# A decoder layer: unit-long score accumulation, row maxima turned through DRAM, and reciprocals of sums spread over partitions by DMA

## The chip, the cores and the metric

One core of one Trainium2 chip runs the whole kernel. The metric is the device time of one execution in microseconds. Beside it the profiler records one execution: its span is the time from the first to the last instruction. The engines are TensorE (PE, with its weight loads PEld), VectorE (DVE), ScalarE (ACT), GpSimd (POOL), and SP, whose queue issues the DMAs.

## The reference

Two sequences of 2048 tokens with 512 features pass through three residual parts. The first is self-attention with 16 heads of 32 features, rotary angles and a softmax over all 2048 keys:

```python
x = x + attn(layernorm(x), W_q, W_k, W_v, W_o)      # softmax(rope(Q) rope(K)^T / sqrt(32)) V, then W_o
x = x + xattn(layernorm(x), ctx, ctx)               # gelu(x ctx^T) ctx, 77 context rows
x = x + clip(layernorm(x) @ sign(W_f)^T * scale + bias, -100, 100)
```

All inputs and outputs are float32.

## The kernel before

**Units, steps, half-steps.** For each batch `project_batch` computes keys, queries and values; then `Attention.run` works through 32 units. A unit is one group `g` of four heads (128 features), one half (256 queries) of a query block `qb`. It has 8 steps; a step takes 256 of the keys (two chunks of 128) for all four heads, and is done in two half-steps of two heads each. The order of TensorE, VectorE, ScalarE and GpSimd within the attention is the one in which the program writes it; SP's order is the scheduler's.

**A half-step on the engines.** TensorE computes the scores of two heads (`scores`, L565), transposed, with keys on partitions, into the banks `st`. Between them it computes plain scores for the *other* two heads of a unit that comes later (`maxima`, L472, three banks `ps`, two used per half-step), which VectorE reduces to row maxima (L484). ScalarE takes the exponential of `st` (L705), GpSimd adds the two chunks (L707), and TensorE multiplies by the values (`weigh`, L583) and, one step later, sums over the keys with a matrix of ones (`total`, L597), both into one bank `acc`. The maxima run `AHEAD` = 10 steps ahead of the scores.

**Scores by differences.** A bank `st` is not cleared from step to step. `lower` (L550) puts the negated row maximum of each query into the bank, as a product of ones with a row `mrow` that holds the maximum in three bfloat16 parts; then step 0 adds the scores of keys in block 0, and each later step adds the product with the *difference* of two key blocks (`dk`), so that the bank holds the new block's scores less the maximum. Steps 0 to 3 do this for the first half of each of the four key blocks, steps 4 to 7 for the second half; so `lower` runs in steps 0 and 4, and clears the banks.

**The maxima's rows.** `split_maxima` takes the negated maximum on VectorE (L491) and splits it in three parts on GpSimd (L493 to L497); `turn_maxima` turns the 128 x 256 tile `mt` with a transposing DMA on SP (L504). For a batch's first unit TensorE turns it (L508).

**Dividing.** `divide` is a generator of which `finish` takes one piece per half-step. After a unit's last totals ScalarE copies `acc` to `num` (L611); VectorE inverts the sums, which stand in 32 equal rows per head, in two pieces of 128 x 128 (L617), and GpSimd multiplies (L620) into the place of the queries. After the last group of a query block, `after_attention` (output projection L382, context part L389 and L408, feed-forward L363, transposes L345) is queued as background, of which a piece is taken at some half-steps.

**Pools.** `work` has 5 tiles of 128 x 512 that `num` shares with the background work; `sums` has 3 tiles `sm`; the angles `cos` and `sin` have their own.

Of the kernel before, what the change touches and what calls it, by code (L numbers as in the profile page):

```python
# [9 lines left out]
F32 = mybir.dt.float32  # L10
F32R = mybir.dt.float32r
BF16 = mybir.dt.bfloat16
# [4 lines left out]
P = 128  # L17
# [11 lines left out]
AHEAD = STEPS + 2  # L29
# [7 lines left out]
def decoder_layer(  # L37
# [51 lines left out]
    cos = const.tile([P, NCH, DK // 2], F32, tag="cos", name="cos")  # L89
    sin = const.tile([P, NCH, DK // 2], F32, tag="sin", name="sin")  # L90
    nc.sync.dma_start(cos, rope_cos.rearrange("(p c) d -> p c d", p=P))
    nc.sync.dma_start(sin, rope_sin.rearrange("(p c) d -> p c d", p=P))
# [13 lines left out]
    mts = []  # L106
    for n in range(2):
        mt = const.tile([P, 2, 4, DK], BF16, tag=f"mt{n}", name=f"mt{n}")
        nc.vector.memset(mt, 0.0)
        mts.append(mt)  # L110
# [69 lines left out]
    def project_batch(b, ahead, att, xnt, wk, wq, wv):  # L180
# [26 lines left out]
        def rotate(ch, a, ps, r):  # L207
            half = [P, H, DK // 2]
            cs = cos[:, ch, None, :, None].to_broadcast(half + [2])
            sn = sin[:, ch, None, :].to_broadcast(half)  # L210
# [234 lines left out]
    class Attention:  # L445
# [53 lines left out]

        def turn_maxima(self, u):  # L500
            mt = mts[u % 2]
            mrow = small.tile([P, 2, P], BF16, tag="mrow", name="mrow")
            if u > 0:
                nc.sync.dma_start_transpose(mrow, mt.rearrange("p c h d -> p (c h d)"))  # L504
            else:
                pt = ps_s.tile([P, 2, P], BF16, tag="s", name="ptm")
                for c in range(2):
                    nc.tensor.transpose(  # L508
                        pt[:, c, :], mt[:, c].rearrange("p h d -> p (h d)"), ident_b
                    )  # L510
                nc.vector.tensor_copy(mrow, pt)
            self.mrow[u] = mrow.rearrange("p c q -> p (c q)")
# [3 lines left out]
        def key_steps(self):  # L516
            self.dk = [None] + [
                const.tile([P, ND, BLK], F32, tag=f"w{n}", name=f"dk{n}") for n in "kqv"
            ]

# [15 lines left out]
            queue.append(others())  # L536

# [21 lines left out]
        def scores(self, u, i, heads, c):  # L559
            qb, g, hf = self.units[u]  # L560
            kb, kc = divmod(self.chunk(i, c), CPB)
            keys = self.dk[kb] if kb else self.k[kb]
            for h in heads:
                r = self.rows[h]
                nc.tensor.matmul(  # L565
                    self.st[h][:, c, :],
                    keys[r, g, kc * P : (kc + 1) * P],
                    self.q[qb][r, g, hf * HQ : (hf + 1) * HQ],
                    start=False,
                    stop=True,  # L570
                    skip_group_check=True,
                )
# [34 lines left out]
        def divide(self, u):  # L607
# [7 lines left out]
            for c in range(2):  # L615
                part = slice(c * P, (c + 1) * P)
                nc.vector.reciprocal(num[:, 1, part], num[:, 1, part])  # L617
                if not last:
                    yield
                (nc.vector if last else nc.gpsimd).tensor_mul(  # L620
                    self.q[qb][:, g, hf * HQ + c * P : hf * HQ + (c + 1) * P],
                    num[:, 0, part],
                    num[:, 1, part],
                )
# [22 lines left out]
        def run(self):  # L647
# [37 lines left out]
            for t in range(NU * STEPS):  # L685
# [12 lines left out]
                for heads, others in (((0, 1), (2, 3)), ((2, 3), (0, 1))):  # L698
                    if i % NB == 0:
                        self.lower(u, heads)  # L700
                    self.scores(u, i, heads, 0)
# [8 lines left out]
                    if heads[0] == 0:  # L710
                        first_half()
                        finish()
                        if u >= NU - ND:
# [3 lines left out]
                    else:  # L717
# [20 lines left out]
    for b in range(B):  # L738
        att = Attention(b)
        project_batch(b, x_next, att, xnt, *qkv)  # L740
# [4 lines left out]
        if b + 1 < B:  # L745
            x_next = att.x_next
            qkv = load_qkv()
    alone.append(True)
# [51 lines left out]
```

## Time and profile before

| | |
|---|---|
| median of 3 runs | 2693.01 us (2692.51 to 2693.29) |
| the profiled execution's own time | 2693.15 us |
| its span | 2691.0 us |
| mean granted TensorE clock | 0.998 |
| TensorE busy | 2668.3 us (99%) |
| VectorE busy | 1710.0 us (64%) |
| ScalarE busy | 1321.0 us (49%) |
| GpSimd busy | 1732.8 us (64%) |
| a unit without background work | 31.09 us |

In the page's groups, the text before the bar names line, engine, operation, output and inputs with their shapes and the count; behind it stand busy time, the mean duration of one in ns, and the engine's idle time before them with what ended it. In a timeline the columns are start and duration in us, engine, line, operation and count. A float32 product is recorded as two instructions. "L" with a number is a line of the kernel before unless said otherwise.

### The profile page before, as it was taken

The numbers are of one execution on the slowest core, as the hardware profiler recorded it, in microseconds if no ns is written. First come the engines' busy times: TensorE is split into PE (matmuls) and PEld (weight loads), VectorE is DVE, ScalarE is ACT, GpSimd is POOL, SyncE is SP. The second block draws the span as 40 slices with busy tenths as digits, with TensorE's granted clock in tenths as the row PEclk, the third lists the DMA queues.
The fourth block names the chain that finished last, engine by engine and source line by source line (L and its number), as shares of the span: only waits on it lengthen the run. The fifth ranks groups of instructions, "written<-read, shape, count | busy, mean of one in ns | idle before, by whom it ended". The sixth has DMA issues, their size and how long they took to land.

```text
span 2691.0 us, 70222 instructions
## 1 busy us (share of the span) xinstructions
PE 2668.3 (99%) x30756; PEld 1490.3 (55%) x30756; DVE 1710.0 (64%) x2863; ACT 1321.0 (49%) x2394; POOL 1732.8 (64%) x1876
## 2 busy tenths in 40 slices
PE   8999999999999999999999999999999999999998
PEld 4445555555555555555554455555565555555555
DVE  3447777676766766676344477766767667766754
ACT  2115555455546554555422155555555455546553
POOL 3227777567857785677543287766687567857772
PEclk9999999999999999999999999999999999999999
DMA  3010000000000000000201000000000000000000
GB/s 126 24 32 2 5 4 4 4 4 18 20 3 4 12 28 3 4 12 26 73 25 40 5 4 4 4 4 4 4 27 12 4 4 19 19 4 4 19 19 17
DMA packets 38019, 43.54 MB, mean 16 GB/s; under 512 B 20662, under 2 KB 20918, under 8 KB 37712
## 3 DMA queue, kind: packets, MB, share of 16 engines
q1 hardware_dynamic: 37712, 39.05, 4.8%
q8 instruction: 241, 3.95, 0.6%
q14 instruction: 66, 0.54, 0.1%
HBM read 26.58 MB, written 8.39 MB: 13 GB/s over the span
## 4 chain that ended last, share of the span: by engine, by line
PE 98%; DVE 1%; DMA 0%; issue 0%; ACT 0%; POOL 0%; SPq 0%; POOLq 0%; ACTq 0%
PE st L565 23%; PE acc L583 22%; PE ps L472 18%; PE acc L597 8%; PE po L382 4%; PE pk L183 4%; PE pq L183 4%; PE pv L183 4%; PE st L550 3%; PE pf L363 2%; PE pt L345 1%; PE po L408 1%; PE ptqk L191 1%; PE ph L389 1%; PE pt L173 1%; DMA wk<-in_wk_t_dram 0%
## 5 line engine op out<-in xcount | busy, mean ns | idle before, releaser
L707 POOL TENSOR_TENSOR sm<-pw 128x512 f32<-128x512 f32 x1024 | 1295.2, 1272 | 599.5 <-ACT pw L705 596.8
L484 DVE TENSOR_REDUCE mx<-ps 128x1 f32<-128x512 f32 x2048 | 1308.9, 682 | 513.0 <-PE ps L472 509.1
L705 ACT ACTIVATE pw<-st 128x512 f32<-128x512 f32 x2048 | 1111.4, 595 | 947.0 <-PE ps L472 619.4
L472 PE MATMUL ps<-k,q 32*128 32x512 f32 x4096 | 1187.8, 640 | 0.0
L583 PE MATMUL acc<-pw,v 128*32 128x256 f32 x8192 | 655.1, 391 | 0.0
L597 PE MATMUL acc<-sm,ones 128*32 128x128 f32 x7680 | 388.8, 280 | 0.0
L583 PEld LDWEIGHTS acc<-pw,v 128*32 128x32 f32 x8192 | 162.5, 108 | 396.6 <-issue 378.3
L472 PEld LDWEIGHTS ps<-k,q 32*128 32x128 f32 x4096 | 352.4, 183 | 20.2 <-issue 13.8
L597 PEld LDWEIGHTS acc<-sm,ones 128*32 128x32 f32 x7680 | 248.6, 110 | 153.2
L565 PE MATMUL st<-q,dkk 32*128 32x256 f32 x2048 | 291.2, 400 | 0.0
L565 PE MATMUL st<-q,dkq 32*128 32x256 f32 x2048 | 290.0, 400 | 0.0
L565 PE MATMUL st<-q,dkv 32*128 32x256 f32 x2048 | 290.0, 400 | 0.0
L565 PE MATMUL st<-q,k 32*128 32x256 f32 x2048 | 262.8, 375 | 0.0
L565 PEld LDWEIGHTS st<-q,dkk 32*128 32x128 f32 x2048 | 175.8, 184 | 89.5 <-issue 51.3
L565 PEld LDWEIGHTS st<-q,dkq 32*128 32x128 f32 x2048 | 173.0, 184 | 79.9 <-issue 54.1
L565 PEld LDWEIGHTS st<-q,dkv 32*128 32x128 f32 x2048 | 175.0, 184 | 58.6 <-issue 26.3
L565 PEld LDWEIGHTS st<-q,k 32*128 32x128 f32 x2048 | 195.4, 187 | 14.0
L219 POOL TENSOR_TENSOR r<-r 128x512 f32<-128x512 f32 x64 | 81.1, 1268 | 161.8 <-DVE r L218 151.5
L617 DVE RECIPROCAL num<-num 128x128 f32<-128x128 f32 x128 | 120.4, 942 | 53.5 <-ACT num L611 53.5
L137 DVE BATCH_NORM_STATS2 st<-x 128x6 f32<-128x512 f32 x96 | 65.4, 686 | 91.7 <-DMA x<-in_x_dram 91.4
L183 PE MATMUL pk<-wk,xnt 128*128 128x512 f32 x256 | 118.2, 606 | 2.4 <-ACT xnt L175 1.3
L382 PE MATMUL po<-wo,q 128*128 128x512 f32 x256 | 117.4, 603 | 0.0
(109 smaller groups left out, 1784.9 us busy)
## 6 DMA issues: line engine op xcount, KB each, us to landing
x<-in_x_dram SPq DMA_DIRECT2D x64, 256.0 KB, 2.8
out_dram<-x SPq DMA_DIRECT2D x32, 256.0 KB, 2.0
wk<-in_wk_t_dram SPq DMA_DIRECT2D x2, 1024.0 KB, 7.8
wq<-in_wq_t_dram SPq DMA_DIRECT2D x2, 1024.0 KB, 9.9
wv<-in_wv_t_dram SPq DMA_DIRECT2D x2, 1024.0 KB, 5.5
wo<-in_wo_t_dram SPq DMA_DIRECT2D x1, 1024.0 KB, 9.9
wf<-in_wf_t_dram SPq DMA_DIRECT2D x1, 1024.0 KB, 5.0
mrow<-mt SPq DMA_TRANSPOSE x62, 2.3
```

The costliest lines, as they stand in the source:

```text
L183: nc.tensor.matmul(dst, xnt[:, i, :], w[:, i, :], start=(i == 0), stop=(i == ND - 1))
L219: nc.gpsimd.tensor_add(r[:, 0, a], r[:, 0, a], r[:, 1, a])
L382: nc.tensor.matmul(ps, ot[:, i, cols], wo[:, i, :], start=(i == 0), stop=(i == ND - 1))
L472: nc.tensor.matmul(ps, self.q[qb][self.rows[h], g, q0 : q0 + P], self.k[kb][self.rows[h], g, :], start=True, stop=True,)
L484: nc.vector.tensor_reduce(mx[:, qc, h, kb : kb + 1], ps, AX.X, ALU.max)
L550: nc.tensor.matmul(self.st[h], ones_b[r, :], mrow[r, None, :].to_broadcast([DK, 2, HQ]), start=True, stop=False, skip_group_check=True,)
L565: nc.tensor.matmul(self.st[h][:, c, :], keys[r, g, kc * P : (kc + 1) * P], self.q[qb][r, g, hf * HQ : (hf + 1) * HQ], start=False, stop=Tr ...
L583: nc.tensor.matmul(acc[self.rows[h], 0, :], self.v[self.chunk(i, c)][:, d0 : d0 + DK], pw[:, h, c, :], start=(i == 0 and c == 0), stop=(i ...
L597: nc.tensor.matmul(acc[self.rows[h], 1, part], ones, sm[:, h, part], start=False, stop=(i == STEPS - 1), skip_group_check=True,)
L617: nc.vector.reciprocal(num[:, 1, part], num[:, 1, part])
L705: nc.scalar.activation(pw[:, h], self.st[h], AF.Exp, scale=SCALE)
L707: nc.gpsimd.tensor_add(sm[:, hs, :], pw[:, hs, 0, :], pw[:, hs, 1, :])
```

## The change

**One `lower` per unit.** Step 4 no longer starts over from block 0: it adds the product with the difference of block 0's second half and the last block's first half. This difference, `wrap` (128 x 256), is made by GpSimd at step 0 of a unit whose group is not the last one's.

**The maxima's rows.** The three parts are made on VectorE, in two pieces, a half-step apart; `mt` shrinks to 128 x 32, VectorE transposes it in 32 x 32 blocks, one DMA stores the result to DRAM, and eight DMAs gather each head's three rows into `mrow`. `AHEAD` becomes 11, and the turning begins five half-steps before the row is used. The first unit still uses TensorE.

**The reciprocals.** Four DMAs spread a row of 256 sums of each head over its 32 partitions (`share`, 128 x 8); three half-steps later VectorE inverts that, four DMAs gather it to one row per head (`once`, a `work` tile), four more spread the row to 32 partitions of `num`, and four half-steps later GpSimd multiplies once. The very last unit divides as before.

**The angles** share a buffer with `sm` (`load_angles`) and are loaded for each batch.

```diff
-AHEAD = STEPS + 2
+AHEAD = STEPS + 3
-    cos = const.tile([P, NCH, DK // 2], F32, tag="cos", name="cos")
-    sin = const.tile([P, NCH, DK // 2], F32, tag="sin", name="sin")
-    nc.sync.dma_start(cos, rope_cos.rearrange("(p c) d -> p c d", p=P))
-    nc.sync.dma_start(sin, rope_sin.rearrange("(p c) d -> p c d", p=P))
+    def load_angles():
+        angles = sums.tile([P, 2, NCH, DK // 2], F32, tag="sm", name="angles")
+        for n, table in enumerate((rope_cos, rope_sin)):
+            nc.sync.dma_start(angles[:, n], table.rearrange("(p c) d -> p c d", p=P))
+        return angles
...
         def split_maxima(self, u):
...
-            mt = mts[u % 2]
-            nc.gpsimd.tensor_copy(mt[:, :, :, 0], neg)
-            nc.gpsimd.tensor_tensor(neg, neg, mt[:, :, :, 0], ALU.subtract)
-            nc.gpsimd.tensor_copy(mt[:, :, :, 1], neg)
-            nc.gpsimd.tensor_tensor(neg, neg, mt[:, :, :, 1], ALU.subtract)
-            nc.gpsimd.tensor_copy(mt[:, :, :, 2], neg)
+            if u == 0:
+                parts = [first_mt[:, :, :, n] for n in range(3)]
+            else:
+                by_head = mts[u % 2][:, :, 0:6].rearrange("p h (c n) -> p c h n", n=3)
+                parts = [by_head[:, :, :, n] for n in range(3)]
+            nc.vector.tensor_copy(parts[0], neg)
+            nc.vector.tensor_tensor(neg, neg, parts[0], ALU.subtract)
+            self.rest = neg, parts
 
         def turn_maxima(self, u):
-            mt = mts[u % 2]
-            mrow = small.tile([P, 2, P], BF16, tag="mrow", name="mrow")
-            if u > 0:
-                nc.sync.dma_start_transpose(mrow, mt.rearrange("p c h d -> p (c h d)"))
+            neg, parts = self.rest
+            nc.vector.tensor_copy(parts[1], neg)
+            nc.vector.tensor_tensor(parts[2], neg, parts[1], ALU.subtract)
+            mrow = mrows[u % 2]
...
+                square = small.tile([P, DK], BF16, tag="square", name="square")
+                nc.vector.transpose(square, mts[u % 2].rearrange("p h n -> p (h n)"))
+                rows = dram.tile([P, DK], BF16, tag="rows", name="rows")
+                nc.sync.dma_start(rows, square)
+                by_row = rows.rearrange("(a h n) i -> n a h i", a=4, h=4)
+                for h in range(4):
+                    for c in range(2):
+                        nc.sync.dma_start(
+                            mrow[h * DK : h * DK + 3, c].rearrange("n (a i) -> n a i", a=4),
+                            by_row[3 * c : 3 * c + 3, :, h, :],
+                        )
...
+        def wrap_around(self, g):
+            if self.wrap is None or self.wrap[0] != g:
+                d = small.tile([P, BLK // 2], F32, tag="wrap", name="wrap")
+                nc.gpsimd.tensor_sub(
+                    d, self.k[0][:, g, BLK // 2 :], self.k[NB - 1][:, g, : BLK // 2]
+                )
+                self.wrap = g, d
...
-            keys = self.dk[kb] if kb else self.k[kb]
+            if i == NB:
+                keys = self.wrap[1][:, None, :].to_broadcast([P, ND, BLK // 2])
+                kc = c
+            else:
+                keys = self.dk[kb] if kb else self.k[kb]
...
         def divide(self, u):
...
-            for c in range(2):
-                part = slice(c * P, (c + 1) * P)
-                nc.vector.reciprocal(num[:, 1, part], num[:, 1, part])
-                if not last:
-                    yield
-                (nc.vector if last else nc.gpsimd).tensor_mul(
...
+                share = small.tile([P, HQ // DK], F32, tag="share", name="share")
+                once = work.tile([P, HQ], F32, tag="w", name="once")
+                for h in range(4):
+                    r = h * DK
+                    nc.sync.dma_start(
+                        share[self.rows[h], :],
+                        num[r : r + 1, 1, :].rearrange("o (j k) -> o j k", j=DK),
+                    )
+                yield
+                yield
+                yield
+                nc.vector.reciprocal(share, share)
+                for h in range(4):
+                    r = h * DK
+                    nc.sync.dma_start(
+                        once[r : r + 1, :].rearrange("o (j k) -> o j k", j=DK),
+                        share[self.rows[h], :],
+                    )
+                    nc.sync.dma_start(
+                        num[self.rows[h], 1, :],
+                        once[r : r + 1, None, :].to_broadcast([1, DK, HQ]),
+                    )
+                yield
+                yield
+                yield
+                yield
+                nc.gpsimd.tensor_mul(out, num[:, 0, :], num[:, 1, :])
...
-                    if i % NB == 0:
+                    if i == 0:
                         self.lower(u, heads)
+                        self.wrap_around(self.units[u][1])
...
                         first_half()
                         finish()
+                        if (t + AHEAD) % STEPS == 0 and u + 1 < NU:
+                            self.turn_maxima(u + 1)
...
                         if (t + AHEAD) % STEPS == STEPS - 1 and u + 1 < NU:
                             self.split_maxima(u + 1)
-                            self.turn_maxima(u + 1)
```

More of the change, by code (lines that the diff above doesn't have):

```diff
@@ L88, in decoder_layer @@
     qkv = load_qkv()
-    cos = const.tile([P, NCH, DK // 2], F32, tag="cos", name="cos")
-    sin = const.tile([P, NCH, DK // 2], F32, tag="sin", name="sin")
-    nc.sync.dma_start(cos, rope_cos.rearrange("(p c) d -> p c d", p=P))
-    nc.sync.dma_start(sin, rope_sin.rearrange("(p c) d -> p c d", p=P))
+    def load_angles():
[3 more added lines that the diff above has]
+        return angles
+    angles = load_angles()
     ident = const.tile([P, P], F32, tag="ident", name="ident")
@@ L103, in decoder_layer, with zeros @@
     nc.scalar.activation(minus_half, ones[:, :CPB], AF.Identity, scale=-0.5)
[L106 to L110, printed above, removed]
+    def zeros(shape, name):
+        t = const.tile(shape, BF16, tag=name, name=name)
+        nc.vector.memset(t, 0.0)
+        return t
+    first_mt = zeros([P, 2, 4, DK], "first_mt")
+    mts = [zeros([P, 4, DK // 4], f"mt{n}") for n in range(2)]
+    mrows = [zeros([P, 2, P], f"mrow{n}") for n in range(2)]
+    dram = ctx.enter_context(tc.tile_pool(name="dram", bufs=2, space=bass.MemoryType.DRAM))
     late = {}
@@ L176, in turn, with project_batch @@
         return xnt
-    def project_batch(b, ahead, att, xnt, wk, wq, wv):
+    def project_batch(b, ahead, att, xnt, angles, wk, wq, wv):
         def times(dst, xnt, w, part=range(ND)):
@@ L208, in rotate @@
             half = [P, H, DK // 2]
-            cs = cos[:, ch, None, :, None].to_broadcast(half + [2])
-            sn = sin[:, ch, None, :].to_broadcast(half)
+            cs = angles[:, 0, ch, None, :, None].to_broadcast(half + [2])
+            sn = angles[:, 1, ch, None, :].to_broadcast(half)
             pairs = ps.rearrange("p (h i t) -> p h i t", i=DK // 2, t=2)
@@ L491, in split_maxima @@
             nc.vector.tensor_reduce(neg, mx, AX.X, ALU.max, negate=True)
-            mt = mts[u % 2]
-            nc.gpsimd.tensor_copy(mt[:, :, :, 0], neg)
-            nc.gpsimd.tensor_tensor(neg, neg, mt[:, :, :, 0], ALU.subtract)
-            nc.gpsimd.tensor_copy(mt[:, :, :, 1], neg)
-            nc.gpsimd.tensor_tensor(neg, neg, mt[:, :, :, 1], ALU.subtract)
-            nc.gpsimd.tensor_copy(mt[:, :, :, 2], neg)
-        def turn_maxima(self, u):
-            mt = mts[u % 2]
-            mrow = small.tile([P, 2, P], BF16, tag="mrow", name="mrow")
-            if u > 0:
-                nc.sync.dma_start_transpose(mrow, mt.rearrange("p c h d -> p (c h d)"))
-            else:
+            if u == 0:
[6 more added lines that the diff above has]
+            self.rest = neg, parts
+        def turn_maxima(self, u):
+            neg, parts = self.rest
+            nc.vector.tensor_copy(parts[1], neg)
+            nc.vector.tensor_tensor(parts[2], neg, parts[1], ALU.subtract)
+            mrow = mrows[u % 2]
+            if u == 0:
                 pt = ps_s.tile([P, 2, P], BF16, tag="s", name="ptm")
@@ L508, in turn_maxima @@
                     nc.tensor.transpose(
-                        pt[:, c, :], mt[:, c].rearrange("p h d -> p (h d)"), ident_b
+                        pt[:, c, :], first_mt[:, c].rearrange("p h d -> p (h d)"), ident_b
                     )
                 nc.vector.tensor_copy(mrow, pt)
+            else:
[10 more added lines that the diff above has]
+                        )
             self.mrow[u] = mrow.rearrange("p c q -> p (c q)")
@@ L519, in key_steps @@
             ]
+            self.wrap = None
             def differences(g):
@@ L561, in scores @@
             kb, kc = divmod(self.chunk(i, c), CPB)
-            keys = self.dk[kb] if kb else self.k[kb]
+            if i == NB:
+                keys = self.wrap[1][:, None, :].to_broadcast([P, ND, BLK // 2])
+                kc = c
+            else:
+                keys = self.dk[kb] if kb else self.k[kb]
             for h in heads:
@@ L614, in divide @@
             last = self.b == B - 1 and u == NU - 1
-            for c in range(2):
-                part = slice(c * P, (c + 1) * P)
-                nc.vector.reciprocal(num[:, 1, part], num[:, 1, part])
-                if not last:
-                    yield
-                (nc.vector if last else nc.gpsimd).tensor_mul(
[L621 to L624, printed above, removed]
+            out = self.q[qb][:, g, hf * HQ : (hf + 1) * HQ]
+            if last:
+                for c in range(2):
+                    part = slice(c * P, (c + 1) * P)
+                    nc.vector.reciprocal(num[:, 1, part], num[:, 1, part])
+                    nc.vector.tensor_mul(out[:, part], num[:, 0, part], num[:, 1, part])
+            else:
+                share = small.tile([P, HQ // DK], F32, tag="share", name="share")
[25 more added lines that the diff above has]
+                nc.gpsimd.tensor_mul(out, num[:, 0, :], num[:, 1, :])
             if g == ND - 1 and (hf == 1 or qb == NB - 1):
@@ L739, in decoder_layer @@
         att = Attention(b)
-        project_batch(b, x_next, att, xnt, *qkv)
+        project_batch(b, x_next, att, xnt, angles, *qkv)
         if b == 0:
@@ L747, in decoder_layer @@
             qkv = load_qkv()
+            angles = load_angles()
     alone.append(True)
```

## The prediction

> **What bounds the kernel now.** I read the page first: engine busy time, the chain that ended last, the cost groups, the DMA issues.
>
> ```profile
> PE 2668.3 (99%) x30756; PEld 1490.3 (55%) x30756; DVE 1710.0 (64%) x2863; ACT 1321.0 (49%) x2394; POOL 1732.8 (64%) x1876
> ...
> PE st L565 23%; PE acc L583 22%; PE ps L472 18%; PE acc L597 8%; PE po L382 4%; PE pk L183 4%; PE pq L183 4%; PE pv L183 4%; PE st L550 3%; PE pf L363 2%; PE pt L345 1%; PE po L408 1%; PE ptqk L191 1%; PE ph L389 1%; PE pt L173 1%; DMA wk<-in_wk_t_dram 0%
> ...
> L484 DVE TENSOR_REDUCE mx<-ps 128x1 f32<-128x512 f32 x2048 | 1308.9, 682 | 513.0 <-PE ps L472 509.1
> ...
> L617 DVE RECIPROCAL num<-num 128x128 f32<-128x128 f32 x128 | 120.4, 942 | 53.5 <-ACT num L611 53.5
> ...
> out_dram<-x SPq DMA_DIRECT2D x32, 256.0 KB, 2.0
> ...
> mrow<-mt SPq DMA_TRANSPOSE x62, 2.3
> ```
>
> TensorE is never idle and the chain is all its lines, so only what shortens or stalls TensorE's own order counts. A busy TensorE can hide a stall, so I then read its timeline in a unit without background work. A unit has 8 steps of two half-steps; each half-step opens with two heads' scores (L565), or with the row of maxima (L550) in steps 0 and 4. The starts of half-steps from step 2 on:
>
> ```profile
> 311.92 0.48 PE L565 MATMUL st<-q,dkq 32*128 32x256 f32 x2
> ...
> 314.13 0.48 PE L565 MATMUL st<-q,dkq 32*128 32x256 f32 x2
> ...
> 316.13 0.48 PE L565 MATMUL st<-q,dkv 32*128 32x256 f32 x2
> ...
> 317.99 0.49 PE L565 MATMUL st<-q,dkv 32*128 32x256 f32 x2
> ...
> 319.89 0.39 PE L550 MATMUL st<-mrow,ones_b 32*128 32x512 bf16 x2
> ...
> 321.86 0.39 PE L550 MATMUL st<-mrow,ones_b 32*128 32x512 bf16 x2
> ...
> 323.83 0.48 PE L565 MATMUL st<-q,dkk 32*128 32x256 f32 x2
> ```
>
> Differences: step 2 takes 2.21 and 2.00 us, step 3 1.86 and 1.90, step 4 (with L550) 1.97 and 1.97. The plain value is 1.86/1.90, so there are two removable things: 0.45 us in step 2 and 0.18 in step 4. The same timeline over all engines, VectorE's rows, says what step 2 is:
>
> ```profile
> 310.75 0.94 DVE L617 RECIPROCAL num<-num 128x128 f32<-128x128 f32 x1
> ...
> 311.61 1.22 DVE L484 TENSOR_REDUCE mx<-ps 128x1 f32<-128x512 f32 x2
> ...
> 312.75 0.94 DVE L617 RECIPROCAL num<-num 128x128 f32<-128x128 f32 x1
> ...
> 313.61 1.22 DVE L484 TENSOR_REDUCE mx<-ps 128x1 f32<-128x512 f32 x2
> ```
>
> Two reduces and a reciprocal are back to back: the half-step's first reduce ends at 311.61 + 0.68 = 312.29, and the second maxima product of the half-step that began at 311.92 needs the bank it frees (three banks, two used per half-step). 0.37 us late, and the half-step is 0.35 too long. In a plain half-step VectorE rests 0.57 us before its reduces:
>
> ```profile
> 334.37 1.29 DVE L484 TENSOR_REDUCE mx<-ps 128x1 f32<-128x512 f32 x2 [0.57 <-PE ps L472]
> ```
>
> So the rule for this kernel: up to 0.57 us of extra VectorE work in a half-step is free; what goes beyond it lengthens TensorE's next half-step one for one.
>
> **The change, part by part.**
>
> *Reciprocals.* Two of 942 ns become one of 128x8. By the slope (942 ns for 128 elements) that is some 60 ns plus a fixed part; I take 0.2 us, below 0.57: free. What the old ones cost, unit by unit on TensorE's timeline: 37 units show 2.22 + 2.00 against 3.76, so 37 x 0.46 = 17.0 us. Eleven more (a transpose L345 or L363 in the half-step before or after) show 0.36 too much: 4.0. Behind the projection L382 and the context product L408 (12 units) the excess is nil. Sum 21 us gained.
>
> *The second row of maxima.* `lower` runs once per unit. Here a rule and a row part.
>
> ```profile
> L550 PE MATMUL st<-mrow,ones_b 32*128 32x512 bf16 x512 | 99.4, 385 | 0.8 <-DVE mrow L511 0.8
> ```
>
> Busy time is 99.4 us for 256 pairs of heads, and half go. The Trainium skill ("TensorE: Matmul & The Clock Gate", Part 3, The mechanism) says that tiles of different row groups overlap and that a weight load overlaps with running products only where the row group differs. By it the two heads' scores, in the same row groups as their L550, wait for all of it: 128 x 0.385 = 49 us gained. By the row of half-steps above it is 0.11 + 0.07 = 0.18 us per unit, 64 x 0.18 = 11.5 us: the scores follow an L550 after 0.21 us and the other two heads' maxima products (L472) run beside both. I take the row: 11.5.
>
> The subtraction for `wrap` (128x256, GpSimd, 40 times, 0.73 us each between the 0.46 of 128 and the 1.27 of 512 columns) fits its idle 0.45 to 0.7 us per half-step, its results being used two steps later; GpSimd also loses five 0.21 us splits per unit.
>
> *One more step ahead.* Each batch computes one more step of maxima before attention, one less in it. In the last steps there are no maxima, and the half-steps are
>
> ```profile
> 2630.19 1.13 PE L565 MATMUL st<-q,dkk 32*128 32x256 f32 x8
> ...
> 2632.04 1.13 PE L565 MATMUL st<-q,dkk 32*128 32x256 f32 x8
> ```
>
> 1.85 us: nothing is saved there (0.05 at most). A step's four products in the projection take 1.07 us (L472 at 1535.02, the next product at 1536.09). Cost 2 x 1.07 = 2.1 us.
>
> *Split and turn on VectorE.* Before: one 0.19 us reduce. Now three tiny operations after one half-step's reduces (negated maximum, copy, difference), three after the next (copy, difference, 32x32 transposes). Near rows: 128x1 and 128x8 operations of 0.15 to 0.19 us, dependent ones starting 0.19 to 0.21 apart. So 0.6 to 0.65 us each time against 0.57: 0.05 late, then 0.12. Some 0.15 us in the 45 units without background there: 6 us. Lower end nothing (0.15 each: 0.5 us, hidden). Upper end 0.3 us each (the 128x256 copy of L511 took 0.29): 0.9 each time, 0.33 + 0.33 late, 45 x 0.66 = 29 us. I take 6, nearest to the small rows.
>
> *The maxima's way through DRAM.* One transposing DMA becomes a store and eight gathers on SP. Issue 0.34 us each (SP's timeline, loads and stores of x), landing 2.0 (store) and 2.3 to 2.8. With a unit's start as zero: the transpose ends in step 5's first half at 19.2 + 2.5 + 0.65 = 22.3; store landed 24.7; the first four gathers (heads 0, 1) issued by 26.1, landed by 28.6; needed at 30.5, the next unit's first half-step. 1.9 us to spare; heads 2 and 3 have the same. The rule that speaks against it is in "DMA: Bandwidth & Descriptors", Specifications: under 512 B the engine does a read-modify-write, and these rows are 64 and 32 B. No row here has such a plain DMA; the nearest is the transposing one at 2.3. I take 2.3 for a hop; the reserve is used up when each of the two takes 3.3.
>
> *The sums' round trip.* Four DMAs spread them, four gather, four broadcast. The copy L611 ends at 5.1 after the unit's start; four issues 1.4 and a landing 2.4: 8.9; the reciprocal stands in VectorE's order at 12.2. Then 1.4 + 2.3, the first broadcast issued at 14.8, the last landed by 18.5; GpSimd's product stands at 21.2. Both have 2.7 us or more; on SP 21 issues take 7.1 of 30.5 us. If the first were late, the reduces behind it on VectorE would wait, and TensorE a half-step later. `num` is held two steps longer and `once` is new among the five work tiles: background work that takes such a buffer waits for it, ScalarE's normalisation nearest, five half-steps (9.4 us) behind a reciprocal whose gather lands after 4; if that cover goes, exponentials queue behind it. SP's stores of x wait for GpSimd's addition: before, those near a unit's end were issued before the copy L611 ended, so the spreading DMAs behind them have no new wait.
>
> *Between the batches.* The angles are loaded again behind the three weights, and wait for the last totals of the first batch (their buffer): issued at about 1329, landed near 1334, where the first rotation stood at 1332.7. VectorE idles there and TensorE does other products first. Batch 0's last unit needs its round trip too, behind the angles: the product lands at about 1342.5, and the fourth projection product of that block, moved behind the values in TensorE's new order, comes up at 1342.2. I take 1 us, range 0 to 4. At the start the angles load in the old place.
>
> **Sum.** -21.0 - 11.5 + 2.1 + 6 + 1 = -23.4. The profiled execution has a span of 2691.0 and took 2693.15, 2.1 around it, and the median of the runs is 2693.01: 2691.0 - 23.4 + 2.1 = 2669.7. I predict 2670.
>
> **The rivals.** A change under 0.2% (5.4 us) can't be told from none.
> (1) *Tiny operations overflow*: 29 in place of 6, 2692.7; halfway 2681. For it: six dependent operations in two half-steps with 0.57 us each. Against: rows of 0.15 to 0.19.
> (2) *Rows late, slower*: if short rows make a hop 4.0 us, the heads' maxima come 1.4 us after 30.5; TensorE waits at the head of nearly each of 62 units: +87, less the gains, 2757. It decides above 3.3 us per hop; with 3.8 it is 1.0 x 62 - 23 = +39, 2732. Against: nothing else is on the queue in most units.
> (3) *Nothing returned from step 2*, because the bank's latency is the next limit: 2691. Against: units behind L382 show 1.86 and 1.90 with their reciprocals hidden. For it: the first unit of a batch has no reciprocal and still shows one 2.11, behind a half-step of only 1.64 without totals.
> (4) *L550 costs more than the half-steps say*, as it also stands in half-steps with background: half of the rule's 49, 24.5 in place of 11.5: 2657.
>
> **How the numbers follow.** Likeliest 0.62 (2664 to 2677); (1) 0.14, half of it beyond 2681; (2) 0.12; (3) 0.06; (4) 0.06. The range 2656 to 2693 leaves out (2) and the edges of the rest. Faster (below 2687.6): 0.62, 0.08 of (1), 0.02 of (3), 0.06 of (4): 0.78. Same: 0.05 of (1), 0.03 of (3): 0.08. Slower: (2) and 0.01 each of (1) and (3): 0.14.
>
> **What would show it.** Right: step 2's half-steps at 1.86 and 1.90, step 4's the same, unit period 30.5 to 30.7 in place of 31.09; VectorE without its 942 ns rows; TensorE's waits for `mrow` by DMA near nothing. Wrong: TensorE's row for `mrow` waiting for DMA at a unit's start (2), steps 5 and 6 longer than 1.9 (1), reciprocals that wait for `share`.

## The result, and the profile after

The changed kernel takes 2776.9 us (median of 4 runs, 2771.6 to 2777.4) against 2692.8 us before (2692.5 to 2693.3): 1.031 times as long, 95% interval 1.029 to 1.033. The forecast was 2670, so the sign is wrong. The profiled execution has a span of 2769.2 us against 2691.0: 78.2 us to explain. It is the shortest of the four (2771.6 us), with a mean granted TensorE clock of 0.994; the other three show 0.991 or 0.992.

The page of the changed kernel: busy time by engine, the chain that ended last, and two of the cost groups.

```profile
PE 2717.6 (98%) x30500; PEld 1475.7 (53%) x30500; DVE 1760.9 (64%) x3121; ACT 1320.8 (48%) x2394; POOL 1694.3 (61%) x1533
...
PE 89%; DVE 8%; POOL 1%; issue 0%; DMA 0%; ACT 0%; SPq 0%; POOLq 0%; ACTq 0%
PE st L605 21%; PE acc L623 19%; PE ps L484 17%; PE acc L637 7%; PE po L394 4%; PE pq L195 4%; PE pk L195 4%; PE pv L195 4%; DVE mx L496 4%; PE pf L375 2%; DVE mt L510 2%; PE st L586 1%; DVE neg L511 1%; PE pt L357 1%; PE po L420 1%; PE ptqk L203 1%
...
L496 DVE TENSOR_REDUCE mx<-ps 128x1 f32<-128x512 f32 x2048 | 1311.6, 683 | 511.4 <-PE ps L484 511.0
...
L484 PE MATMUL ps<-k,q 32*128 32x512 f32 x4096 | 1240.0, 642 | 26.2 <-DVE mx L496 26.2
```

The same line of the page before:

```profile
PE 98%; DVE 1%; DMA 0%; issue 0%; ACT 0%; POOL 0%; SPq 0%; POOLq 0%; ACTq 0%
```

VectorE's share of the chain has grown from 1% to 8%, and the chain now names two operations on eight numbers per partition, L510 and L511. Of the new DMAs it holds one wait, at the end of the first batch's attention, and no reciprocal. TensorE's maxima products (L484) wait 26 us for VectorE's reduces; before, the idle column of that row is 0.0.

Next TensorE's timeline in a unit without background (the scores' rows that open each half-step; the end of one line's half-step is the start of the next).

```profile
316.38 0.48 PE L605 MATMUL st<-q,dkq 32*128 32x256 f32 x2
...
318.24 0.48 PE L605 MATMUL st<-q,dkq 32*128 32x256 f32 x2
...
320.13 0.48 PE L605 MATMUL st<-q,dkv 32*128 32x256 f32 x2
...
323.89 0.48 PE L605 MATMUL st<-q,wrap 32*128 32x256 f32 x2
...
325.75 0.48 PE L605 MATMUL st<-q,wrap 32*128 32x256 f32 x2
...
327.64 0.48 PE L605 MATMUL st<-q,dkk 32*128 32x256 f32 x2
...
329.50 0.48 PE L605 MATMUL st<-q,dkk 32*128 32x256 f32 x2
...
330.80 0.69 PE L484 MATMUL ps<-k,q 32*128 32x512 f32 x1 [0.17 <-DVE mx L496]
...
332.64 0.48 PE L605 MATMUL st<-q,dkq 32*128 32x256 f32 x2
```

Step 2 takes 1.86 and 1.89 us (before 2.21 and 2.00) and step 4 takes 1.86 and 1.89 (before 1.97 and 1.97): both gains are there. But one half-step of step 5, from 329.50 to 332.64, takes 3.14 us instead of 1.90. A clean unit (one without background work) should then take 31.09 - 0.46 - 0.18 + 1.24 = 31.69 us, and the period from one copy of the sums to the next is 31.69. VectorE's rows in that stretch, and GpSimd's:

```profile
320.62 0.19 DVE L675 RECIPROCAL share<-share 128x8 f32<-128x8 f32 x1
...
328.24 0.19 DVE L504 TENSOR_REDUCE neg<-mx 128x8 f32<-128x32 f32 x1
328.46 1.02 DVE L510 CAST mt<-neg 128x8 bf16<-128x8 f32 x1
329.51 0.63 DVE L511 TENSOR_TENSOR neg<-neg,mt 128x8 f32<-128x8 f32 x1
330.07 1.27 DVE L496 TENSOR_REDUCE mx<-ps 128x1 f32<-128x512 f32 x2
```

```profile
328.17 1.27 POOL L774 TENSOR_TENSOR sm<-pw 128x512 f32<-128x512 f32 x1 [0.46 <-ACT pw L772]
329.40 0.72 POOL L690 TENSOR_TENSOR q<-num 128x256 f32<-128x256 f32 x1
```

The copy of eight numbers begins at 328.46 and ends at 329.48; GpSimd's addition of the exponentials ends at 329.44. The difference begins at 329.51 and ends at 330.14; GpSimd's product ends at 330.12. The reduce L504 begins inside the same addition and takes 0.19. Of the 62 copies at L510, 60 take 0.45 us or more, and all 60 end 0.04 to 0.05 us behind the end of a GpSimd instruction.

The rows of L510 and L511 have a control in them: the first unit of each batch runs the same two operations while GpSimd stands still (durations are min/median/max in ns).

```profile
L510 DVE CAST mt<-neg x62: 296/1023/1241, 233.5 to 2680.0; 128x8 bf16<-128x8 f32 x62
L510 DVE CAST first_mt<-neg x2: 184/184/185, 212.2 to 1582.2; 128x8 bf16<-128x8 f32 x2
...
L511 DVE TENSOR_TENSOR neg<-neg,mt x62: 170/636/1189, 234.6 to 2681.0; 128x8 f32<-128x8 f32 x62
L511 DVE TENSOR_TENSOR neg<-neg,first_mt x2: 171/172/172, 212.5 to 1582.5; 128x8 f32<-128x8 f32 x2
```

That gives theory A: a VectorE copy, or a VectorE operation with two SBUF inputs, is held until GpSimd's running instruction ends, and that is the whole loss. Theory B, the rival: the new DMAs and the longer queue cost the time, mostly in units with background, and the small operations only add to the clean ones. For B speaks that units with background lost too: a period of eight units takes 295 us against 283.6, and 11 us is more than eight times 0.6.

### The profile page after: what moved, and what is told of

It reads as the page before. It is cut to its first block, busy times and chain, and to the rows that moved or that the text cites. A ratio compares the mean times of both kernels' runs of the same rounds, so it can differ in the third digit from the quotient of the medians.

```text
span 2769.2 us, 72066 instructions
## 1 busy us (share of the span) xinstructions
PE 2717.6 (98%) x30500; PEld 1475.7 (53%) x30500; DVE 1760.9 (64%) x3121; ACT 1320.8 (48%) x2394; POOL 1694.3 (61%) x1533
## 4 chain that ended last, share of the span: by engine, by line
PE 89%; DVE 8%; POOL 1%; issue 0%; DMA 0%; ACT 0%; SPq 0%; POOLq 0%; ACTq 0%
PE st L605 21%; PE acc L623 19%; PE ps L484 17%; PE acc L637 7%; PE po L394 4%; PE pq L195 4%; PE pk L195 4%; PE pv L195 4%; DVE mx L496 4%; PE pf L375 2%; DVE mt L510 2%; PE st L586 1%; DVE neg L511 1%; PE pt L357 1%; PE po L420 1%; PE ptqk L203 1%
## 5 line engine op out<-in xcount | busy, mean ns | idle before, releaser
L484 PE MATMUL ps<-k,q 32*128 32x512 f32 x4096 | 1240.0, 642 | 26.2 <-DVE mx L496 26.2
L484 PEld LDWEIGHTS ps<-k,q 32*128 32x128 f32 x4096 | 356.8, 183 | 93.6 <-DVE mx L496 79.6
L605 PE MATMUL st<-q,dkk 32*128 32x256 f32 x2048 | 306.7, 406 | 0.0
L605 PE MATMUL st<-q,wrap 32*128 32x256 f32 x1024 | 144.9, 400 | 0.0
L605 PE MATMUL st<-q,k 32*128 32x256 f32 x1024 | 131.6, 374 | 0.0
L149 DVE BATCH_NORM_STATS2 st<-x 128x6 f32<-128x512 f32 x96 | 65.0, 682 | 92.6 <-DMA x<-in_x_dram 92.3
L339 DVE TENSOR_TENSOR x<-po,x 128x512 f32<-128x512 f32 x64 | 44.2, 690 | 122.6 <-PE po L394 94.2
```

Of the source, the lines that this page charges most:

```text
L149: nc.vector.bn_stats(st, xc)
L484: nc.tensor.matmul(ps, self.q[qb][self.rows[h], g, q0 : q0 + P], self.k[kb][self.rows[h], g, :], start=True, stop=True,)
L605: nc.tensor.matmul(self.st[h][:, c, :], keys[r, g, kc * P : (kc + 1) * P], self.q[qb][r, g, hf * HQ : (hf + 1) * HQ], start=False, stop=Tr ...
```

## The experiments

**GpSimd in VectorE's place.** The four operations go back to GpSimd, where the kernel before has them; nothing else is touched. The first two, and the two of `parts[1]` and `parts[2]` alike:

```
-            nc.vector.tensor_copy(parts[0], neg)
-            nc.vector.tensor_tensor(neg, neg, parts[0], ALU.subtract)
+            nc.gpsimd.tensor_copy(parts[0], neg)
+            nc.gpsimd.tensor_tensor(neg, neg, parts[0], ALU.subtract)
...
```

> The changed kernel with its two copies and two differences of the maxima put back on GpSimd; all else (DRAM detour, sums' round trip, wrap, one more step ahead, the 32x32 transposes on VectorE) stays. Theory A (VectorE's copy and difference are held until GpSimd's running instruction ends, and this is the whole loss): clean unit 30.5 to 30.8 us instead of 31.69, step 5's half-steps at 1.9, total 2665 to 2690. Theory B (the loss is in the DMA round trips and the longer queue, the small operations only add to clean units): the clean unit falls to about 31.0 but the units with background stay at 36 to 40, total 2730 to 2750.

Measured: 2827.5 us, 1.050 times the time before (1.0485 to 1.0516), slower than the changed kernel; clean unit 32.14. Neither theory said that. The mean granted clock is 0.985 here, against 0.998 before, so part of the loss is clock. GpSimd's and VectorE's rows of the unit say why.

```profile
330.74 0.73 POOL L690 TENSOR_TENSOR q<-num 128x256 f32<-128x256 f32 x1
331.41 0.22 POOL L510 CAST mt<-neg 128x8 bf16<-128x8 f32 x1
...
333.39 0.23 POOL L517 TENSOR_TENSOR mt<-neg,mt 128x8 bf16<-128x8 f32 x1
...
333.65 0.21 DVE L528 STREAM_TRANSPOSE square<-mt 128x32 bf16<-128x32 bf16 x1 [2.21 <-POOL mt L517]
...
334.49 0.69 PE L484 MATMUL ps<-k,q 32*128 32x512 f32 x1 [0.62 <-DVE mx L496]
```

The transposes stand on VectorE ahead of the half-step's reduces. GpSimd reaches the splits only behind its addition and its product, so VectorE waits 2.21 us in order, and TensorE behind it. The edit brought a new wait of its own and decides nothing between A and B; a later version (below) takes it away.

**The copies in another form.** Each copy is written as a reduction over one element: same engine, place, input and output.

```
-            nc.vector.tensor_copy(parts[0], neg)
+            nc.vector.tensor_reduce(parts[0], neg[:, :, :, None], AX.X, ALU.max)
...
-            nc.vector.tensor_copy(parts[1], neg)
+            nc.vector.tensor_reduce(parts[1], neg[:, :, :, None], AX.X, ALU.max)
```

> The changed kernel, each copy to bfloat16 written as a reduction over one element on VectorE (same input, same output, another form); the differences stay. Theory A in its narrow form (only some forms are held: copies, and operations with two SBUF inputs; the reduce L504 is not): L510 falls from 1.02 to about 0.19 us, the difference L511 then starts inside the addition L774 and is held to its end, some 0.8 us, the pair ends 0.7 us earlier, step 5's long half-step 3.14 becomes about 2.45, total about 2735. Theory A in its wide form (any small VectorE operation is held): no change, 2777. Theory B: no change.

Measured: 2731.7 us (1.0149 times before, 1.0132 to 1.0166), 45 us less than the changed kernel; the long half-step is 2.46.

```profile
326.16 0.19 DVE L504 TENSOR_REDUCE neg<-mx 128x8 f32<-128x32 f32 x1
326.38 0.19 DVE L510 TENSOR_REDUCE mt<-neg 128x8 bf16<-128x8 f32 x1
326.61 0.78 DVE L511 TENSOR_TENSOR neg<-neg,mt 128x8 f32<-128x8 f32 x1
```

The copy falls from 1.02 to 0.19 by its form alone; the difference, with its two inputs, now starts inside the addition (326.09 to 327.36) and is held to 327.39. This is what theory A says in its narrow form (only some forms are held), and the expected 0.19, 0.8 and 2.45 us came.

**GpSimd's product elsewhere.** Two more half-steps before L690; VectorE's instructions are those of the changed kernel.

```
                 yield
+                yield
+                yield
                 nc.gpsimd.tensor_mul(out, num[:, 0, :], num[:, 1, :])
```

> The changed kernel with GpSimd's product L690 two half-steps later. Theory A: the cast L510 still ends with the addition L774 (1.02 us), but the difference L511 then finds GpSimd idle and takes 0.17 to 0.2 us instead of 0.63; the long half-step 3.14 becomes about 2.7, clean unit 31.25, total about 2750. If L511 is long by itself, it stays at 0.63 and the total at 2777.

Measured: 2757.7 us (1.0242, 1.0227 to 1.0258), 19 less than the changed kernel. VectorE's rows:

```profile
328.61 1.02 DVE L510 CAST mt<-neg 128x8 bf16<-128x8 f32 x1
329.67 0.17 DVE L511 TENSOR_TENSOR neg<-neg,mt 128x8 f32<-128x8 f32 x1
...
330.95 0.69 DVE L516 CAST mt<-neg 128x8 bf16<-128x8 f32 x1
```

L511 falls to 0.17 with nothing changed on VectorE, so its 0.63 was GpSimd's product. The clean unit is 31.58 where 31.25 was expected: the half-step is 2.68, as forecast, but the second copy, L516, now begins 0.62 us into the next addition and is held in turn (the next half-step is 2.25).

**The split on VectorE, in the kernel before.** Only the engine of the split changes; the DMA that transposes, the reciprocals and both rows of maxima stay.

```
-            nc.gpsimd.tensor_copy(mt[:, :, :, 0], neg)
-            nc.gpsimd.tensor_tensor(neg, neg, mt[:, :, :, 0], ALU.subtract)
+            nc.vector.tensor_copy(mt[:, :, :, 0], neg)
+            nc.vector.tensor_tensor(neg, neg, mt[:, :, :, 0], ALU.subtract)
...
```

> The kernel before with nothing changed but that the copies and differences of the maxima run on VectorE instead of GpSimd (four operations behind the reduce, all in one half-step). Theory A: the first copy is held to the end of GpSimd's addition, about 1.0 us, the other three 0.2 each if GpSimd is then idle, up to 1 us more if it isn't: 1.8 us or more against 0.57 free, 62 times 1.2 = 75 us slower, about 2768 or above. By the sizes of the prediction (0.2 us each, 1.0 in all, 0.43 late): 2720.

Measured: 2809.5 us, 117 slower than before (1.0428, 1.0413 to 1.0444). None of the changed kernel's new DMAs is in it, so theory B has nothing to explain this with. In a clean unit the first copy alone is held, and the unit takes 32.30 us, 1.21 more than before. In five of the 62 units GpSimd had the next instructions ready, and one operation after the other waited for one more of them:

```profile
1623.99 1.02 DVE L493 CAST mt<-neg 128x8 bf16<-128x8 f32 x1
1625.05 1.18 DVE L494 TENSOR_TENSOR neg<-neg,mt 128x8 f32<-128x8 f32 x1
1626.26 1.20 DVE L495 CAST mt<-neg 128x8 bf16<-128x8 f32 x1
```

Not all of the 117 us is the hold itself: the mean granted clock is 0.986, against 0.998 before, an estimate of some 34 us (0.012 of 2807.5).

**Which forms are held.** The kernel before, with an additional 128x8 operation on VectorE in some half-steps, on tiles of its own. A first version put it directly behind the reduces.

> The kernel before with one extra 128x8 operation on VectorE after the reduces of each second half-step, a different form in each of the eight steps, on tiles that nothing else uses: copy to bfloat16, copy, difference of two SBUF tiles, reduction over one element, product with a constant, the same to bfloat16, reciprocal, fill. It starts 0.1 to 0.3 us into GpSimd's addition of 1.27 us. Theory A: the copy to bfloat16 and the difference take about 1.0 us and end with the addition; the reduction and the reciprocal 0.19; the other four tell which forms are held. If smallness or position matters and not the form: all eight alike. The time itself: 64 units by the held ones, about 0.5 us late each, 2730 to 2830.

Measured: 2751.6 us. It misses its purpose: most of the operations began 0.04 to 0.07 us before GpSimd's addition did, and those ran their 0.15 to 0.2 us undisturbed beside it; only the float32 copy began inside one as a rule (median 1.20 us, to its end). So the one that starts first is not held. The second version put two small reductions ahead.

> The kernel before with an extra 128x8 operation on VectorE after the reduces of each half-step, behind two small reductions that put its start some 0.3 us inside GpSimd's addition; eight forms, each in two of a unit's sixteen half-steps. Theory A: copy to bfloat16 and difference are held to the end of GpSimd's running instruction (0.8 to 1.0 us), the reduction and the reciprocal take 0.15 to 0.2; the rest (one-input product with a constant to float32 and to bfloat16, two-input product and difference, fill) tells whether it is the second input, the copy or the output type. If the form is not what matters, all are alike. No time is expected of it but a longer one.

Measured: 2857.4 us. The rows of the eight forms (the line numbers tell them apart: copy to bfloat16, product and difference with two inputs, difference, reduction, product with a constant to float32 and to bfloat16, reciprocal, fill):

```profile
L125 DVE CAST p_half<-p_in x128: 159/1142/2120, 216.3 to 2784.6; 128x8 bf16<-128x8 f32 x128
L127 DVE SCALAR_TENSOR_TENSOR p_out<-p_in,p_two x128: 149/344/1262, 219.8 to 2786.2; 128x8 f32<-128x8 f32 x128
L129 DVE TENSOR_TENSOR p_out<-p_in,p_two x128: 147/157/1295, 223.6 to 2787.5; 128x8 f32<-128x8 f32 x128
L131 DVE TENSOR_REDUCE p_out<-p_in x128: 144/151/163, 227.4 to 2788.2; 128x8 f32<-128x8 f32 x128
L133 DVE TENSOR_SCALAR p_out<-p_in x128: 159/704/1236, 214.9 to 2785.8; 128x8 f32<-128x8 f32 x128
L135 DVE TENSOR_SCALAR p_half<-p_in x128: 155/993/1721, 217.7 to 2786.4; 128x8 bf16<-128x8 f32 x128
L137 DVE RECIPROCAL p_out<-p_in x128: 181/188/195, 221.6 to 2788.0; 128x8 f32<-128x8 f32 x128
L139 DVE MEMSET p_out<- x128: 65/65/65, 226.0 to 2788.4; 128x8 f32 x128
```

Two kinds: five forms have maxima over 1.2 us, three never leave their own duration. The rest follows from the start of each instance against GpSimd's rows, over the whole trace. Of those that began more than 0.05 us inside one of GpSimd's additions or products, with at least 0.25 us of it left, all 77 copies, all 64 and 20 two-input operations and all 71 and 67 products with a constant were held. Each ended 0.02 to 0.03 us behind a GpSimd instruction: behind that one, or, in 13 cases, behind the next, which followed at once. Of 67 reductions, 67 reciprocals and 63 fills none was held.

GpSimd's instruction matters too. Five of the copies and products with a constant began inside its one-input clip of 128x512 (L404, 1.9 us) or its power of 128x1; none was held to the end of it (two copies took 0.54 us, the three products 0.16). In the first probing kernel eight differences ran in 0.16 us inside the same clip, near its end. Why is open.

**The split in reductions alone.** The changed kernel, split still on VectorE. A difference becomes a negated copy beside the number and a sum over the pair; seven reductions and the transposes stand in three half-steps instead of two.

```
+            both = [small.tile([P, 2, 4, 2], F32, tag=f"both{n}", name=f"both{n}") for n in range(2)]
+            nc.vector.tensor_reduce(both[0][:, :, :, 0], mx, AX.X, ALU.max, negate=True)
+            nc.vector.tensor_reduce(parts[0], both[0][:, :, :, 0:1], AX.X, ALU.max)
...
+            nc.vector.tensor_reduce(both[0][:, :, :, 1], parts[0][:, :, :, None], AX.X, ALU.max, negate=True)
+            nc.vector.tensor_reduce(both[1][:, :, :, 0], both[0], AX.X, ALU.add)
+            nc.vector.tensor_reduce(parts[1], both[1][:, :, :, 0:1], AX.X, ALU.max)
...
```

> The changed kernel with the split of the maxima still on VectorE, but written in reductions alone, which have one input: a copy is a reduction over one element, a difference is a negated copy and a sum over the pair; seven reductions and the transpose stand in three half-steps (2, 3 and 3 of them, 0.4 to 0.65 us each time). Theory A (only copies and two-input operations are held by GpSimd): each takes 0.17 to 0.2 us, no half-step of a clean unit is over 1.90 but the last of the unit, clean unit 30.4 to 30.5 us, total 2660 to 2675: the gains of the prediction arrive. If the small operations are held whatever their form, or the DMA detour (now one half-step later) costs: 2730 or more.

Measured: 2678.4 us, 0.9948 times the time before (0.9933 to 0.9963). More operations on VectorE, and 98.5 us less than the changed kernel. The clean unit is 30.45. The form and the third half-step came together here, so this run does not part them; the form alone was worth 45 us for the two copies above.

```profile
325.67 0.16 DVE L516 TENSOR_REDUCE both<-mt 128x8 f32<-128x8 bf16 x1
325.87 0.17 DVE L517 TENSOR_REDUCE both<-both 128x8 f32<-128x16 f32 x1
326.07 0.19 DVE L518 TENSOR_REDUCE mt<-both 128x8 bf16<-128x8 f32 x1
```

**GpSimd, without the wait.** The first experiment again, with all four operations directly behind the reduce L504, the product two half-steps later, and the transposes one half-step later.

```
+            nc.gpsimd.tensor_copy(parts[0], neg)
+            nc.gpsimd.tensor_tensor(neg, neg, parts[0], ALU.subtract)
+            nc.gpsimd.tensor_copy(parts[1], neg)
+            nc.gpsimd.tensor_tensor(parts[2], neg, parts[1], ALU.subtract)
...
```

> The changed kernel with the split on GpSimd, all four operations in the half-step of the reduce, GpSimd's product two half-steps later and the 32x32 transposes on VectorE one half-step later, so that they needn't wait for GpSimd. If the 2827 of the first GpSimd version came from the transposes that stood on VectorE ahead of the reduces and waited for GpSimd (2.2 us per unit), this version has clean units of 30.4 to 30.6 us and a total of 2662 to 2680. If GpSimd itself is too full (0.46 to 0.75 us idle per half-step, the four take 0.85 and gaps), the additions come late, exponentials' buffers with them, and it stays above 2700.

Measured: 2683.9 us (0.9966, 0.9952 to 0.9979), clean unit 30.45. The changed kernel's DMAs are all in it and in the version before it, the maxima's one half-step later, and both are faster than the kernel before. So theory B falls as the cause of the loss.

**The other parts, each alone on the kernel before.** First the sums' round trip:

```
+                    nc.sync.dma_start(
+                        share[self.rows[h], :],
+                        num[r : r + 1, 1, :].rearrange("o (j k) -> o j k", j=DK),
+                    )
...
+                nc.vector.reciprocal(share, share)
...
```

> The kernel before with the sums' round trip alone (spread by DMAs, one small reciprocal, gathered and broadcast, one product); everything else as before. By the prediction: -21 us, 2672; half-steps of step 2 at 1.86 and 1.90; the split of the maxima stays on GpSimd. If the round trip itself harms (GpSimd's product, the buffers held longer in units with background): less than 10 us gained.

Measured: 2679.2 us against 2692.8, 13.6 less (0.995, 0.9933 to 0.9967). Then the second row of maxima (with the angles loaded per batch, as the changed kernel has them):

```
-                    if i % NB == 0:
+                    if i == 0:
                         self.lower(u, heads)
+                        self.wrap_around(self.units[u][1])
...
```

> The kernel before with the second row of maxima taken out alone (the wrap-around difference on GpSimd, and the angles loaded per batch to make room for it); reciprocals, the split and the transposing DMA stay. By the prediction: half-steps of step 4 at 1.86 and 1.90, clean unit 31.09 - 0.18 = 30.91, total 11.5 less and about 1 more between the batches: 2682. By the rule of the row groups 49 less: 2645. If only clean units gain: 45 x 0.18 = 8 less, 2685.

Measured: 2682.9 us against 2692.0, 9.1 less (0.9965, 0.9951 to 0.9978); clean unit 30.91, as expected.

**The step ahead.** The one-input version keeps 14.3 us of the 22.7 that these two give alone. The end of the projection in the changed kernel's second batch, TensorE's timeline, shows where some of the rest is:

```profile
1575.95 1.14 PE L484 MATMUL ps<-k,q 32*128 32x512 f32 x8
1577.86 2.32 PE L484 MATMUL ps<-k,q 32*128 32x512 f32 x8 [0.76 <-DVE mx L496]
1580.11 5.40 PE L195 MATMUL pv<-wv,xnt 128*128 128x512 f32 x8
```

Two steps' products now follow each other. The second waits for the reduces of the first, four of 0.68 us against 1.07 for the products, and the eight products behind it, 3.70 us before, take 5.40: TensorE's granted clock in those 5.40 us is 0.68. The edit moves one of the two steps into an earlier chunk (and the angles ahead of the third weight).

```
+            if ch == NCH - 3:
+                att.lead(1)
             background_between(2)
...
```

> The one-input version (2678.4) with the steps of maxima that are computed ahead spread evenly (one of them moved from the end of the projection, where two follow each other, to its third chunk from the end), and the angles loaded ahead of the third weight. The trace of the changed kernel shows the second of the two steps waiting for VectorE's reduces and, in the second batch, TensorE's clock at 0.66 to 0.69 for the 5 us behind that wait; if that is what the step ahead costs above its 1.07 us, 2 us come back in the first batch and 3.7 in the second: about 2672. If not, 2678.

Measured: 2676.8 us (0.9943, 0.9929 to 0.9956); 15.2 less than the kernel before timed beside it, where the one-input version was 14.3 less than its own; the intervals of the two overlap. Both waits and the slow products are gone, and the stretch between the batches is 2.8 us shorter, but the first batch reaches its first sums 1.3 us later. Why is open; the weights' changed order of loading is a candidate that was not tried alone.

**Everything but the maxima's way.** The two parts together on the kernel before; split, transposing DMA and ten steps ahead as they were.

> The changed kernel without the maxima's way through DRAM: the kernel before with the sums' round trip (2679.2 alone) and without the second row of maxima (2682.9 alone), the split on GpSimd and the transposing DMA and the ten steps ahead as before. If the two gains add (-13.5 and -9.1, each measured alone), 2670, with clean units at 31.09 - 0.46 - 0.18 = 30.45; then the detour and its extra step ahead cost the one-input version 8 us, although its clean units are 30.45 as well. If GpSimd, which keeps the split and gets the wrap-around difference and the whole product, is too full, 2676 or above.

Measured: 2672.4 us (0.9923, 0.991 to 0.9937), 20.6 less than before; clean unit 30.45. It has the lowest median of all versions. Its interval and that of the one-input version (0.9933 to 0.9963) meet at the edge, so that the 6 us between them are likely but not certain.

## Why the prediction was wrong

**The step that failed** is "Split and turn on VectorE", 6 us with an upper end of 29. By the span it cost 92.6 us (2769.2 against 2676.6 of the one-input version), by the medians 98.5. I had sized six operations by the rows nearest in size, 128x1 and 128x8 at 0.15 to 0.19, "0.3 us each" at most. The 128x8 rows are reductions, and the 128x1 rows of two inputs or a constant did not run beside one of GpSimd's additions. What was put at 0.2 us each is held by GpSimd: summed over the 62 units that go through DRAM, the four copies and differences take 62.9, 40.2, 17.0 and 18.2 us, together 138 where 248 times 0.19 would be 47. The prediction's rule then does the rest: in the clean unit L504, L510 and L511 fill 1.93 us behind the reduces, 0.57 are free, and the half-step is 1.24 too long. The clock has a part in it, too: the last section finds about 12 us.

The profile before held a warning: GpSimd is busy 64% of the time, and each half-step's addition begins about when VectorE's reduces end (within 0.1 us in the first of the two probing kernels), which is where the change puts the operations. It even has the hold itself, once. One two-input operation on two numbers per partition began inside an addition and took 1.24 us; nine of the same line with one number, none beside an addition, took 0.16:

```profile
1289.79 1.28 POOL L707 TENSOR_TENSOR sm<-pw 128x512 f32<-128x512 f32 x1
1289.85 1.24 DVE L148 TENSOR_TENSOR stats<-stats 128x2 f32<-128x2 f32 x1 [4.21 <-POOL stats L147]
```

The prediction does not name this row. A page stated the rule, which I had not weighed: the Trainium skill, "SBUF — State Buffer", Who interferes with whom, says that VectorE and GpSimd share a pair of ports, that it is held for a whole instruction and the later one blocks; that copies, casts and products with a constant can take it; that operations with two SBUF inputs contend with a GpSimd instruction that reads SBUF; and that reductions never do. Beside GpSimd's additions and products the runs agree in every form that was tried, with the hold's end 0.02 to 0.05 us behind GpSimd's, and show reciprocal and fill free; beside the clip, which reads SBUF too, none was held to its end. By that rule the copy could have been costed at up to the addition's 1.27 us and the difference at up to the product's 0.73: an estimate of 0.19 + 1.27 + 0.73 - 0.57 = 1.6 us late per unit, 73 us in the prediction's 45 units, and the forecast would have been slower.

The rival "Tiny operations overflow" named the right place, but with 29 us at its upper end it came out level with before.

**The other steps.** The rule that VectorE's excess over 0.57 us lengthens TensorE's next half-step one for one held to 0.14 us in the clean unit of four runs: an excess of 1.36 gave 1.24 in the changed kernel, 1.35 gave 1.21 with the split on VectorE in the kernel before, 0.69 gave 0.56 with the copies as reductions, 0.92 gave 0.78 with the product later.

*One row of maxima fewer*: predicted 11.5 less about 1 between the batches, measured 9.1; the row, not the rule of the row groups (49), was right.

*Reciprocals*: the clean unit gains its 0.46 exactly (31.09 to 30.63), but the whole gains 13.6, not 21. Eight units of a block gain 1.98 us in place of 2.6 (21 us over 64 units, times eight), although the first background unit is 4.1 us shorter: the next is 3.1 longer (42.10 and 35.53 become 37.99 and 38.67), three of the others are 0.3 longer and one is 1.2 shorter. Background work starts some half-steps later, behind the longer way of the sums. That the later start is the cause is argued, not shown. The stretch between the batches is 1.4 longer, of which TensorE waits 1.2 once, in the output projection (L382), for the last unit's late product.

*One more step ahead*: 2.1 predicted. Against the version without detour the one-input version is 1.6 us later at its first sums and 4.1 us longer between the batches, 5.7 of the 6.3 that separate their spans. Two steps in a row make TensorE wait 0.76 us for VectorE in each batch, which the 1.07 us of the products left out; as spreading them brought little on balance, the rest is open.

*Between the batches*: the angles cost nothing that the runs show (249.7 us from sums to sums before, 249.4 with angles and wrap); in the changed kernel the last unit's round trip made TensorE wait 1.1 us once, about the 1 us forecast.

*Rows late*, the rival that was to decide the sign: no wait of TensorE for a DMA at a unit's start; the row store was issued at 331.99 and the first gather, which waits for its landing, at 333.47, so a hop is 1.5 us, not 2.3 and far from 3.3.

*The sums' round trip* stayed hidden but for that one wait, though its four spreading issues take 2.42 us and not 1.4.

## What to carry to other kernels

A small VectorE operation that starts inside one of GpSimd's additions or products costs what is left of that instruction, if it is a copy, a product with a constant or an operation with two SBUF inputs. Beside GpSimd's clip and power this did not show. So cost it by its form and by what GpSimd runs at that moment, not by its size; where it is on the way of the bounding engine, write it as a reduction, or start it before GpSimd's instruction. And try the parts of a change alone: all of this one's parts but the maxima's rows were worth 20.6 us together, and the rows' new way took that and 84 us more.

## What the runs showed that was not expected

TensorE's granted clock fell behind some short waits. In the changed kernel a maxima product waited once 0.94 us in a unit with background, and the next five microseconds ran at 0.67 (columns: window; its length, then busy time by engine, granted clock, DMA share, GB/s).

```profile
719.17 0.69 PE L484 MATMUL ps<-k,q 32*128 32x512 f32 x1 [0.94 <-DVE mx L496]
```

```profile
716.00:719.90 3.90, 2.96 (x34) 1.03 (x28) 3.80 (x7) 1.09 (x2) 3.90 (x4) 1.00 0.18 67
719.90:725.00 5.10, 5.10 (x54) 2.75 (x56) 3.17 (x6) 2.17 (x4) 2.94 (x3) 0.67 0.21 54
```

That is 5.1 times 0.33, 1.7 us lost on top of the wait. In windows of 5 us between 200 and 2640, the changed kernel has six such places, about 12 us in all; the kernel before has none, and the one-input version one. The wait alone does not decide it. In that stretch of the changed kernel L484 waited 0.92 us or more 20 times and 0.76 us twice; the clock fell behind five of the 20 and one of the two. The half-steps of 3.14 us in clean units, in which TensorE's rows show only 0.17 us of waiting, are followed by no such place. What decides is open.
